# Turning blocks of the adjacency mask by DMA instead of on TensorE, with the mask applied in two VectorE operations

## The chip, the cores and the metric

The kernel runs on one core of a Trainium2 chip. The metric is the device time of one execution in microseconds. TensorE (PE) multiplies matrices and turns tiles; VectorE (DVE), ScalarE (ACT) and GpSimd (POOL) work elementwise; SyncE (SP) has no arithmetic and issues DMAs. Each engine runs its own list of instructions in order; semaphores tie the lists together.

## The reference, cut to what matters

Sixteen graphs of 1024 nodes with 128 features each go through two layers. The first is a gated graph network of four steps: messages by the adjacency matrix, then a GRU cell on every node, and a normalised residual. The second is a GraphSAGE network of three layers on a *thinned* adjacency matrix, and another normalised residual. The thinning is sequential by rows:

```python
def step(carry, n):
    row = jnp.take(carry, n, axis=0)
    num = jnp.sum(row); sf = jnp.where(num > 10, (num + 1) // 2, 1)
    rank = jnp.cumsum(row)
    rm = row & (rank % sf == 0)        # nothing is removed where num <= 1
    carry = carry.at[n].set(row & ~rm)
    carry = carry.at[:, n].set(carry[:, n] & ~rm)   # the same entries of column n
    return (carry, None)
```

What row n removes at column m is also removed at row m, column n. So row m needs, before its own entries are ranked, everything that earlier rows removed in column m.

## The kernel before, in words

The first stage, some 1290 us of the 2233, does two things side by side. `Gated` runs the gated network in two streams of graphs (a stream per parity) and its layers call a function `aside` at fixed places; each call lets `FixPoint.steps` go on to its next `yield`. So the order in which the two jobs' instructions stand on each engine is written out by hand: nothing moves when a duration changes. The rest of the time is the three GraphSAGE layers (`Sage`), which read the thinned adjacency.

`FixPoint` thins four graphs at a time (G = 4). A *round* i is one block of 128 rows, k = 0 to 7, of these four graphs; 32 rounds make the stage, and two layers of `Gated` pass in each. For a round, GpSimd has loaded the four row blocks as `f_a` (128 x 1024, bf16). Then:

- `turn` (L719) brings what older row blocks removed in these columns. For older blocks 0 to k-2 that comes back from HBM: `read_back` (L708) has read the 128x128 blocks into `f_rt` one round earlier, on SP's queue, and TensorE turns each of them (L726) into `f_tr`, which is in PSUM. Block k-1 was made in this round and is still in SBUF as `f_nr` (`fresh`), and is turned in the same way. All k blocks of a graph go to the same columns of `f_tr`, graph after graph.
- `keep` (L728) multiplies `f_a` by the sign of the turned blocks, in one VectorE `scalar_tensor_tensor` (L731) over k x 128 columns with one input in PSUM.
- `count` (L734) is a running sum along the row (L739), then parameters, three guesses of what is removed within the diagonal block (L893, L900, L908), and in the next round the final `f_nr` of all 1024 columns (L870, L872), stored to `e_nr` in HBM (L873).

The four calls of `turn` and `keep` in a round stand at fixed steps; the four `read_back` for the next round are called between those for graphs 2 and 3. Buffers: `f_rt` has 4 (pool `f_rts`), `f_tr` is one PSUM tile of one bank whose last 128 columns also hold small numbers.

Beside this, TensorE runs `Gated`'s message matmuls (L1096, on `h_a`, the adjacency that GpSimd's queue loads) and gate matmuls (L1108), and turns h (L1041); VectorE combines gates (L1121, L1123, L1136) and checks a loaded block `h_test` (L998, L1992); GpSimd multiplies gates (L1131, L1135, L1137) and issues the loads of `f_a` (L687).

Of the kernel before, what the change touches and what calls it, by code (L numbers as in the profile page):

```python
# [9 lines left out]
BF = mybir.dt.bfloat16  # L10
# [5 lines left out]
ALU = mybir.AluOpType  # L16
# [5 lines left out]
P = 128  # L22
# [3 lines left out]
NB = N // P  # L26
# [29 lines left out]
class Dilate:  # L56
# [152 lines left out]
    def steps(self):  # L209

        for b in range(B):
            self.load(0, b)
            yield 3.0
        for k in range(NB):
            self.start_chain(k)
            for t in range(P):
                self.chain_step(k, t)
                yield 1.9
            self.end_chain(k)
            x = {}  # L220
            for i in range(B + 3):
                if i < B:
                    x[i] = self.rank(k, i)
                if 1 <= i <= B:
                    self.remove(k, i - 1, x.pop(i - 1))
                if i >= 3 and k + 1 < NB:
                    self.load(k + 1, i - 3)
                yield 5.0
# [402 lines left out]
class FixPoint:  # L631
# [76 lines left out]
    def read_back(self, i, g):  # L708

        if i >= len(self.todo) or self.todo[i][0] < 2:  # L710
            return
        k, b0 = self.todo[i]
        k1 = k - 1
        rt = self.rts.tile([P, NB - 2, P], BF, name="f_rt")
        self.nc.sync.dma_start(rt[:, :k1, :], self.not_r[b0 + g, :k1 * P, k * P:k * P + P]
                               .rearrange("(j p) n -> p j n", p=P))
        self.left[i, g] = rt

    def turn(self, i, g):  # L719

        k = self.todo[i][0]
        if k:
            rt = self.left.pop((i, g), None)
            for j in range(k):
                src = rt[:, j, :] if j < k - 1 else self.fresh[g][:, k * P:k * P + P]
                self.nc.tensor.transpose(self.tr[:, j, :], src, self.cst["ident_b"])  # L726

    def keep(self, i, a):  # L728
        k = self.todo[i][0]
        if k:  # L730
            self.nc.vector.scalar_tensor_tensor(a[:, :k * P], self.tr[:, :k, :].rearrange("p k n -> p (k n)"),  # L731
                                                0.0, a[:, :k * P], op0=ALU.is_ge, op1=ALU.mult)

    def count(self, i, g, a, rank, other):  # L734
        nc = self.nc
# [6 lines left out]
    def steps(self):  # L742

        nc, G = self.nc, self.G
        for c in range(G):
            self.load(c)
        old = None
        for i, (k, b0) in enumerate(self.todo):
            diag = slice(k * P, k * P + P)

            yield
            if old:
                old.settle()
                old.wide_u(0)
            yield
            if old:
                old.wide_u(1)
                old.rows(0)
            yield
            if old:  # L760
                old.wide_u(2)
                old.rows(1)
            yield
            if old:
                old.rows(2)
                old.wide_u(3)
                old.rows(3)
            a = [self.loaded.pop((i, g)) for g in range(G)]
            pt = self.ps.tile([P, G, P], F32, name="f_pd")
            turned = pt.rearrange("p g n -> p (g n)").bitcast(BF)[:, :G * P].rearrange("p (g n) -> p g n", g=G)  # L770
            for g in range(G):
                nc.tensor.transpose(turned[:, g, :], a[g][:, diag], self.cst["ident_b"])
            yield
            if old:
                old.last_u()

            both = self.small.tile([P, G, P], BF, name="f_both")
            for g in range(G):
                nc.vector.tensor_mul(both[:, g, :], a[g][:, diag], turned[:, g, :])
            nc.gpsimd.affine_select(both, both, pattern=[[0, G], [1, P]], compare_op=ALU.is_gt, fill=0.0,  # L780
                                    base=0, channel_multiplier=-1)
            self.turn(i, 0)
            yield
            rank = self.two.tile([P, G, N], F16, name="f_rank")
            self.keep(i, a[0])
            self.count(i, 0, a[0], rank, pt)
            yield
            yield
            self.turn(i, 1)
            self.keep(i, a[1])  # L790
            yield
            self.count(i, 1, a[1], rank, pt)
            if i == 0:

                for c in range(G, self.LOTS):
                    self.load(c)
            yield
            yield
            yield
            self.turn(i, 2)  # L800
            self.keep(i, a[2])
            self.count(i, 2, a[2], rank, pt)
            yield
            for g in range(G):
                self.read_back(i + 1, g)
            yield
            self.turn(i, 3)
            self.keep(i, a[3])
            self.count(i, 3, a[3], rank, pt)

            num = self.sm[:, 0, 0, :]
            nc.vector.tensor_scalar(num, rank[:, :, N - 1], 1.0, None, op0=ALU.mult)
            q = self.params(num, 0)
            u = self.diag_u(rank[:, :, diag], q)
            if old:
                old.check()
                for g in range(G):
                    self.load(G * (i - 1) + g + self.LOTS)
            yield
            x = self.removed(u, q, both)  # L820
            yield
            yield
            pd, num = self.less(x, rank, 1)
            rd = self.small.tile([P, G, P], F16, name="f_rd")
            q = self.params(num, 1, lambda: nc.vector.tensor_sub(rd, rank[:, :, diag], pd))
            u = self.diag_u(rd, q)
            yield
            x = self.removed(u, q, both)
            yield
            old = self.Block(self, i, a, rank, both, x)  # L830
            yield
        yield
        old.settle()
        for n in range(4):
            old.wide_u(n)
            if n < 3:
                yield
            old.rows(n)
        yield
        old.last_u()  # L840
        yield
        old.check()
# [81 lines left out]
class Gated:  # L924
# [215 lines left out]
    def run(self, steps):  # L1140

        streams = [self.stream(s) for s in range(2)]
        first, second = streams
        first.load_x(first.b)
        self.load_weights()
        next(steps)
        for j in range(NB):
            first.load_adj(first.b, j)
        first.begin_rows(first.b)
        self.prepare()  # L1150
        second.load_x(second.b)
        for j in range(NB):
            second.load_adj(second.b, j)

        first.begin(0)
        for n in range(9):
            next(steps)
        for b0 in range(0, B, 2):
            for l in range(L0):
                for s in range(2):  # L1160
                    st, ot = streams[s], streams[1 - s]
                    self.layer(st, l, self.beside(st, ot, l, s, b0, steps))
        last = streams[1]
        for f in range(2):
            last.finish(f)
        for _ in steps:
            pass
# [910 lines left out]
```

## Time and profile before

| | |
|---|---|
| Median of 3 runs | 2233.61 us (2232.93 to 2242.04) |
| The profiled execution, its own time | 2232.83 us |
| Its span, first to last instruction | 2230.8 us |
| TensorE busy | 2129.7 us (95%) |
| VectorE busy | 1926.9 us (86%) |
| ScalarE busy | 1327.2 us (59%) |
| GpSimd busy | 1082.6 us (49%) |
| L726 on TensorE, `f_rt` and `f_nr` | 336 and 112 instructions |
| L731 on VectorE | 112 instructions, 265 to 1083 ns |
| L715 on SP's queue | 96 DMAs, 32 to 192 KB |

Lines of the profile name an engine, a kernel line, an operation and what it writes and reads (`out<-in`, with partitions x elements and type). A number in brackets is the idle time of the engine just before, and the arrow what ended it. A busy TensorE is not TensorE at its peak, as the ends of matmuls are modelled; the distance of starts is the surer measure.

### The profile page before, as it was taken

To read this page: it belongs to the slowest core of one execution; us is meant where nothing else is said; L and a number is where in the kernel's file an instruction comes from. 1 tells how busy PE (TensorE), PEld (TensorE's weight loads), DVE (VectorE), ACT (ScalarE), POOL (GpSimd) and SP (SyncE) were. 2 spreads that over 40 slices of the span, in tenths; PEclk is the share of its full clock that TensorE was granted. 3 is DMA by queue.
4 is the path that set the end of the run, shared out by engine and by line. 5 is a ranking of instruction groups with operands and counts; after the bars stand their busy time and mean duration, and the time that the engine had idled before them with its cause. 6 is when DMAs were issued, how large, how long until landed. Compare 5 with 4: busy or idle time off the path is not lost. (4 is left out here: it accounts for less than half of the span.)

```text
span 2230.8 us, 33341 instructions
## 1 busy us (share of the span) xinstructions
PE 2129.7 (95%) x10665; PEld 1456.6 (65%) x10665; DVE 1926.9 (86%) x4338; ACT 1327.2 (59%) x3238; POOL 1082.6 (49%) x1092
## 2 busy tenths in 40 slices
PE   6999999999999999999999979999999899998987
PEld 4566655666656666555665557777777678887865
DVE  4999999999998999999999978888888766666877
ACT  3657557565565656556566465666666455556756
POOL 4347437356355364364463346777777344551002
PEclk9999999999999999999999989999999999999989
DMA  8247347347356265364383259888888577765404
GB/s 251 71 103 240 80 114 229 71 120 214 86 156 177 73 200 138 90 201 118 73 264 85 64 184 329 305 305 297 305 301 304 169 259 260 257 221 174 152 29 144
DMA packets 214396, 402.46 MB, mean 180 GB/s; under 512 B 59586, under 2 KB 80740, under 8 KB 214212
## 3 DMA queue, kind: packets, MB, share of 16 engines
q1 hardware_dynamic: 168388, 280.68, 37.3%
q0 software_dynamic: 41472, 117.46, 19.3%
q10 hardware_dynamic: 4352, 2.11, 0.4%
q8 instruction: 86, 1.41, 0.3%
q14 instruction: 98, 0.80, 0.1%
HBM read 324.49 MB, written 109.25 MB: 194 GB/s over the span
## 5 line engine op out<-in xcount | busy, mean ns | idle before, releaser
L1108 PE MATMUL h_g<-h_h,h_wh 128*128 128x512 f32 x768 | 399.2, 601 | 3.1 <-DVE h_r L1121 3.1
L1108 PE MATMUL h_g<-h_ms,h_wi 128*128 128x512 f32 x768 | 392.1, 592 | 0.0
L739 DVE TENSOR_TENSOR_SCAN f_rank<-f_a,f_first,f_pd 128x1024 f16<-128x1024 bf16 x128 | 299.2, 2343 | 3.3
L1137 POOL TENSOR_TENSOR h_h<-h_zh,h_r 128x512 f32<-128x512 f32 x126 | 205.3, 1629 | 195.2 <-DVE h_r L1136 172.2
L1096 PE MATMUL h_g<-h_a,h_hi 128*128 128x512 f32 x1024 | 282.8, 417 | 2.2 <-DMA h_a<-in_adj_dram 2.0
L1108 PEld LDWEIGHTS h_g<-h_ms,h_wi 128*128 128x128 f32 x768 | 145.6, 190 | 183.9 <-issue 166.8
L1096 PE MATMUL h_g<-h_a,h_lo 128*128 128x512 f32 x1024 | 264.1, 395 | 0.0
L1513 POOL CAST p_b<-p_at 128x512 uint8<-128x512 f32 x256 | 219.4, 879 | 84.2 <-DVE p_at L1505 59.8
L1096 PEld LDWEIGHTS h_g<-h_a,h_hi 128*128 128x128 f32 x1024 | 188.4, 188 | 63.8 <-issue 20.1
L1096 PEld LDWEIGHTS h_g<-h_a,h_lo 128*128 128x128 f32 x1024 | 190.0, 188 | 39.4
L1406 ACT ACTIVATE s_junk<-s_o 128x128 bf16<-128x128 f32 x384 | 114.0, 298 | 170.7 <-DVE s_o L1399 170.7
L1131 POOL TENSOR_TENSOR h_zh<-h_z,h_h 128x512 f32<-128x512 f32 x63 | 80.1, 1271 | 275.5 <-ACT h_z L1127 275.5
L1108 PEld LDWEIGHTS h_g<-h_h,h_wh 128*128 128x128 f32 x768 | 129.2, 190 | 85.9 <-issue 65.5
L1099 ACT COPY h_ms<-h_g 128x512 f32<-128x512 f32 x128 | 73.8, 577 | 183.3 <-PE h_g L1096 139.3
L1124 ACT ACTIVATE h_r<-h_r,h_bi 128x512 f32<-128x512 f32 x128 | 92.3, 721 | 131.2 <-DVE h_r L1123 131.1
L916 ACT ACTIVATE f_u<-f_rank,f_q 128x128 f16<-128x128 f16 (+7 forms) x128 | 110.6, 867 | 74.9 <-DVE f_rank L856 74.9
L1992 DVE SCALAR_TENSOR_TENSOR p_junk<-p_a 128x1024 bf16<-128x1024 f32 x96 | 125.7, 1309 | 0.0
L893 ACT ACTIVATE f_pd<-f_rank,f_q 128x128 f32<-128x128 f16 x128 | 59.1, 461 | 109.8 <-DVE f_q L701 106.6
L1781 PE MATMUL q_ob<-s_wxp,q_xt 128*128 128x256 f32 x512 | 123.4, 385 | 0.3
L1505 DVE SCALAR_TENSOR_TENSOR p_at<-p_nr,p_u 128x128 fp32r<-128x128 bf16 (+1 forms) x192 | 102.5, 543 | 20.5 <-ACT p_at L1497 15.0
L1492 PE MATMUL p_u<-ident_b,p_nr 128*128 128x128 bf16 x1024 | 97.2, 224 | 7.2 <-DVE p_at L1505 5.0
L1423 POOL TENSOR_TENSOR q_rl<-s_r,q_rh 128x512 fp32r<-128x512 f32 x32 | 41.1, 1285 | 128.0 <-ACT q_rh L1422 105.5
(260 smaller groups left out, 4946.3 us busy)
## 6 DMA issues: line engine op xcount, KB each, us to landing
h_a<-in_adj_dram POOLq DMA_DIRECT2D x128, 512.0 KB, 9.5
p_a<-in_adj_dram SPq DMA_DIRECT2D x96, 512.0 KB
f_a<-in_adj_dram POOLq DMA_DIRECT2D x128, 256.0 KB, 6.6
e_nr<-f_nr SPq DMA_DIRECT2D x128, 256.0 KB
p_nr<-e_nr SPq DMA_DIRECT2D x32, 1024.0 KB
h_test<-in_adj_dram SPq DMA_DIRECT2D x32, 512.0 KB
s_at<-p_b SPq DMA_DIRECT2D x32, 512.0 KB
s_ag<-s_ag SPq DMA_DIRECT2D x64, 256.0 KB
```

The source lines that it names most:

```text
L739: nc.vector.tensor_tensor_scan(out, a, other[:, 0, 0:1].to_broadcast([P, N]), start, op0=ALU.add, op1=ALU.bypass)
L916: nc.scalar.activation(u[:, :n1], rank[:, g, :n1], AF.Abs, bias=q[:, 1, g:g + 1], scale=q[:, 0, g:g + 1])
L1096: nc.tensor.matmul(pm[f], part[:, j, :], st.adj[j][:, half[f]], start=(j == 0 and n == 0), stop=(j == NB - 1 and n == 1))
L1108: nc.tensor.matmul(pg, lhs, rhs, start=(i == 0), stop=(i == len(mm) - 1))
L1124: nc.scalar.activation(r, r, AF.Tanh, bias=bias(self.bi, 2))
L1137: aid.tensor_tensor(h, zh, r, ALU.subtract)
L1406: self.nc.scalar.activation(junk, o[:, i, :], AF.Square, accum_out=ss[:, i:i + 1])
L1492: nc.tensor.matmul(pu[:, i * P:(i + 1) * P], v[:, 4 * f + i, j * P:(j + 1) * P], self.cst["ident_b"], start=True, stop=True)
L1505: self.nc.vector.scalar_tensor_tensor(g["at"][:, j, c0:c0 + low], v[:, j, c0:c0 + low], 0.0, pu[:, :low], op0=ALU.is_lt, op1=ALU.is_lt)
L1513: self.nc.gpsimd.tensor_copy(g["b", f][:, j, :], g["at"][:, j, f * HF:(f + 1) * HF].bitcast(F32))
L1781: nc.tensor.matmul(pb[:, i], g["xt"][:, f, blk], self.wxp, start=(i % 2 == 0), stop=False)
L1992: nc.vector.scalar_tensor_tensor(junk, a, 0.0, a, op0=ALU.is_gt, op1=ALU.not_equal, accum_out=bad[:, c:c + 1])
```

## The change

The older blocks are turned on their way from HBM: `read_back` issues one transposing DMA per graph from SP, which writes the k-1 blocks to `f_rt` already turned. TensorE turns only block k-1, into a slot of `f_tr` of its own per graph. `keep` applies the mask in two operations: columns of blocks 0 to k-2 with `f_rt` in SBUF as the second input, columns of block k-1 with `f_tr` in PSUM. Rounds with k = 0 and 1 have no older blocks. In the changed file the kernel's lines from here on stand one lower.

```diff
         k1 = k - 1
-        rt = self.rts.tile([P, NB - 2, P], BF, name="f_rt")
-        self.nc.sync.dma_start(rt[:, :k1, :], self.not_r[b0 + g, :k1 * P, k * P:k * P + P]
-                               .rearrange("(j p) n -> p j n", p=P))
+        rt = self.rts.tile([P, (NB - 2) * P], BF, name="f_rt")
+        self.nc.sync.dma_start(rt[:, :k1 * P], self.not_r[b0 + g, :k1 * P, k * P:k * P + P], transpose=True)
         self.left[i, g] = rt

     def turn(self, i, g):

         k = self.todo[i][0]
         if k:
-            rt = self.left.pop((i, g), None)
-            for j in range(k):
-                src = rt[:, j, :] if j < k - 1 else self.fresh[g][:, k * P:k * P + P]
-                self.nc.tensor.transpose(self.tr[:, j, :], src, self.cst["ident_b"])
-
-    def keep(self, i, a):
-        k = self.todo[i][0]
+            self.nc.tensor.transpose(self.tr[:, g, :], self.fresh[g][:, k * P:k * P + P], self.cst["ident_b"])
+
+    def keep(self, i, g, a):
+        k, stt = self.todo[i][0], self.nc.vector.scalar_tensor_tensor
         if k:
-            self.nc.vector.scalar_tensor_tensor(a[:, :k * P], self.tr[:, :k, :].rearrange("p k n -> p (k n)"),
-                                                0.0, a[:, :k * P], op0=ALU.is_ge, op1=ALU.mult)
+            last = slice((k - 1) * P, k * P)
+            if k > 1:
+                rt = self.left.pop((i, g))
+                stt(a[:, :(k - 1) * P], rt[:, :(k - 1) * P], 0.0, a[:, :(k - 1) * P], op0=ALU.is_ge, op1=ALU.mult)
+            stt(a[:, last], self.tr[:, g, :], 0.0, a[:, last], op0=ALU.is_ge, op1=ALU.mult)
...
-            self.keep(i, a[0])
+            self.keep(i, 0, a[0])
```

The other three calls of `keep` change in the same way.

More of the change, by code (lines that the diff above doesn't have):

```diff
@@ L789, in steps @@
             self.turn(i, 1)
-            self.keep(i, a[1])
+            self.keep(i, 1, a[1])
             yield
@@ L800, in steps @@
             self.turn(i, 2)
-            self.keep(i, a[2])
+            self.keep(i, 2, a[2])
             self.count(i, 2, a[2], rank, pt)
@@ L807, in steps @@
             self.turn(i, 3)
-            self.keep(i, a[3])
+            self.keep(i, 3, a[3])
             self.count(i, 3, a[3], rank, pt)
```

## The prediction

> **What bounds the kernel now.** I read the page's 40 slices first: TensorE is busy 90% or more in every slice of the first 1290 us (the stage that the change touches), but VectorE stands at 9 there too. A busy share can't separate two engines that are both full, so I cut one group of four graphs into its eight rounds (k = 0 to 7). Each window starts where the round's L772 transposes start on TensorE.
>
> ```profile
> 655.20:696.00 40.80, 40.16 (x157) 24.47 (x156) 36.33 (x70) 27.45 (x58) 34.09 (x38) 1.00 0.84 271
> 696.00:734.40 38.40, 38.40 (x146) 23.13 (x146) 36.42 (x78) 22.85 (x42) 14.79 (x14) 1.00 0.30 72
> 734.40:773.00 38.60, 38.60 (x150) 23.33 (x150) 36.45 (x78) 22.39 (x41) 14.29 (x14) 1.00 0.30 76
> 773.00:811.80 38.80, 38.80 (x154) 23.54 (x154) 36.99 (x78) 22.29 (x41) 16.42 (x18) 1.00 0.47 132
> 811.80:852.70 40.90, 40.90 (x173) 25.17 (x172) 37.39 (x74) 28.08 (x61) 33.48 (x38) 1.00 0.89 283
> 852.70:892.40 39.70, 39.48 (x161) 24.01 (x160) 38.37 (x78) 22.62 (x42) 14.72 (x14) 1.00 0.34 83
> 892.40:932.40 40.00, 39.73 (x166) 24.25 (x166) 38.63 (x78) 22.39 (x41) 14.47 (x14) 1.00 0.35 86
> 932.40:972.90 40.50, 40.19 (x170) 24.39 (x170) 39.20 (x76) 22.36 (x40) 16.54 (x18) 1.00 0.40 117
> ```
>
> Columns: window, its length, then busy us of TensorE, its weight loads, VectorE, ScalarE, GpSimd, clock, DMA share, GB/s. To see: at k = 1, 2, 3 the length is TensorE's busy time. By the L772 starts (696.01, 734.38, 772.97, 811.79) these rounds take 38.37, 38.59 and 38.82 us, so one more row block costs 0.22 to 0.23. In k = 5, 6, 7 (39.69, 39.97, 40.49) the length is above TensorE's line (38.37 + 0.23 each would give 39.29, 39.52, 39.75), TensorE idles 0.2 to 0.3 us, and VectorE idles only 1.33, 1.37 and 1.30 us, which is the sum of small gaps between some 78 instructions. There VectorE sets the length. So the stage has two owners: TensorE to k = 4, VectorE from k = 5.
>
> What a transpose really costs is the distance of starts, in the TensorE timeline of round 6, not its 220 ns:
>
> ```profile
> 902.51 0.44 PE L726 MATMUL f_tr<-ident_b,f_rt 128*128 128x128 bf16 x5
> 902.79 0.22 PE L726 MATMUL f_tr<-ident_b,f_nr 128*128 128x128 bf16 x1
> 902.85 0.65 PE L1108 MATMUL h_g<-h_h,h_wh 128*128 128x512 f32 x1
> ```
>
> Six take 902.85 - 902.51 = 0.34 us: 57 ns each, and 4 x 57 = 0.23 us per row block, the step found above.
>
> The mask on VectorE, from the groups by shape:
>
> ```profile
> L731 DVE SCALAR_TENSOR_TENSOR f_a<-f_tr,f_a 128x768 bf16<-128x768 bf16 x16 | 15.1, 941 | 0.0
> L731 DVE SCALAR_TENSOR_TENSOR f_a<-f_tr,f_a 128x128 bf16<-128x128 bf16 x16 | 4.5, 280 | 1.4 <-PE f_tr L726 1.2
> L886 DVE SCALAR_TENSOR_TENSOR f_junk<-f_x 128x512 f16<-128x512 bf16 x31 | 21.5, 692 | 1.1
> ```
>
> (941 - 280) / 640 = 1.03 ns an element, plus 0.147 us fixed. L886 is the same operation with both inputs in SBUF: 692 ns for 512, against 680 for L731 at 512 from PSUM. Neither the place nor the 16-bit type makes it cheaper.
>
> A second cost, of place. L1992 is one instruction in two stages, from the answer for its tile and line; below it the third mask of round 6 and GpSimd beside it:
>
> ```profile
> L1992 DVE SCALAR_TENSOR_TENSOR p_junk<-p_a x96: 1204/1214/1831, 1334.0 to 1775.3; 128x1024 bf16<-128x1024 f32 x96
> L1992 DVE SCALAR_TENSOR_TENSOR h_junk<-h_test x32: 1626/1644/2171, 58.1 to 1290.3; 128x1024 bf16<-128x1024 f32 x32
> 908.85 1.29 POOL L1135 TENSOR_TENSOR h_zh<-h_z,h_h 128x512 f32<-128x512 f32 x1
> 909.92 0.93 DVE L731 SCALAR_TENSOR_TENSOR f_a<-f_tr,f_a 128x768 bf16<-128x768 bf16 x1
> 910.23 1.29 POOL L1137 TENSOR_TENSOR h_h<-h_zh,h_r 128x512 f32<-128x512 f32 x1
> ```
>
> In the first stage the least L1992 takes 1626 ns instead of 1204: it starts 0.4 us before a GpSimd L1135 ends, each time. The mask at 909.92 has one input in PSUM and pays nothing beside the same L1135.
>
> Last, SP's queue in round 6:
>
> ```profile
> 894.22 3.94 SPq L873 DMA_DIRECT2D e_nr<-f_nr  x4
> 898.28 14.96 SPq L715 DMA_DIRECT2D f_rt<-e_nr  x4
> 913.28 0.54 SPq L998 DMA_DIRECT2D h_test<-in_adj_dram  x1
> ```
>
> The reads for round 7 go out one by one as their buffers come free and are used 39 us later; h_test is behind them on the queue.
>
> **What the Trainium skill says.** "SBUF — State Buffer", Who interferes with whom: a VectorE instruction with two SBUF inputs and a GpSimd instruction that reads SBUF exclude each other for the whole instruction; with one SBUF input there is no contention. The trace agrees (1626 against 1204). "Vector Engine (DVE) Microarchitecture Reference", Performance modes, lists copy, cast, tensor_scalar and tensor_tensor for the packed modes and not scalar_tensor_tensor; L886 at 692 ns agrees. "DMA: Bandwidth & Descriptors", Queues, rings and completion order: each DMA engine takes a queue's descriptors in ring order; no row here shows it by itself. Prices of a DMA transpose: 1309 ns for 128x128 bf16 ("VectorE: DVE Perf Modes", The three transpose paths) and 261 GB/s (the DMA page, Latency and other measured facts). This trace has no DMA transpose.
>
> **The change part by part**, per round k >= 2, four graphs each.
>
> *TensorE* loses 4 x (k - 1) transposes: 0.23, 0.46, 0.69, 0.92, 1.15, 1.38 us for k = 2 to 7. Over the stage 336 x 57 ns = 19.2 us, which is a gain only where TensorE sets the length.
>
> *VectorE* gets a second operation per mask. Elements stay; the fixed part comes once more, 0.147 us, less the overlap of two independent operations: two L1136 of 0.684 us take 1.28, so 0.083. Four times 0.064 = 0.26 us. The first of the two has both inputs in SBUF: the third graph's mask always meets L1135 (909.92 against 908.85 + 1.29 = 910.14), wait 0.22 us. Sum 0.48 us a round. Bounds: 0.26 if the port costs nothing; 1.36 if nothing overlaps (0.59), the port costs 0.22 and one L687 issue of 0.55 us on GpSimd, which runs beside the fourth mask, shuts it out too. A gain from SBUF input is excluded by L886. I take 0.48, as each term has a row.
>
> *GpSimd's* L1137, pushed back by the third mask's 0.7 us, holds the second half of h, which TensorE turns (L1041) some 8 us later: hidden.
>
> *Waits.* The SBUF mask waits for the DMA transpose; behind it on VectorE are the scan L739 and L1121/L1123, which free the PSUM banks that TensorE's L1108 needs. SP's L715 waits for the mask instead of the transposes: 898.28 becomes about 901.3, the last about 914; behind it stand h_test and, far later, L873. TensorE's remaining transposes still wait for the mask before, as all write one bank. SP and GpSimd issue as many DMAs in the same order as before.
>
> *DMA.* A round-7 transpose moves 192 KB: 0.75 us at 261 GB/s, 7.9 us at 1309 ns per 128x128 block. Deadlines are 39 us off; four take 3 or 31 us. I take the low end as likelier, since a single small transfer's time needn't add up over blocks, and keep the high one for a rival.
>
> *Sum by round*, larger of the two engines (VectorE: busy + 1.33 + 0.48): k = 2: 38.26 against 38.37, so -0.22. k = 3: 38.80, so -0.02. k = 4: VectorE 39.20, TensorE 40.94 - 0.69, so -0.69. k = 5, 6, 7: +0.48 each, +1.44. A group +0.51 us, four groups **+2.0 us**. The profiled execution took 2232.8 (span 2230.8, 2.0 outside) and would take 2234.8; the median of the runs is 0.8 higher: **2236**.
>
> **Rivals.** *DMA transposes at 1309 ns a block.* Round 7's 24 take 31.4 us from 901.3, to 932.7; h_test behind them, 512 KB at the page's 180 GB/s, lands at 935.6, and VectorE's L1992 wants it at about 930.1 (37.7 us after the round's start, as in round 5). 5.5 us late, 22 in all: 2258. Where DMA is 0.89 busy (k = 4) another 21 us of transposes could hold up the h_a loads, up to 16 us a group: 2323. I put it at 2265. It decides from 1.08 us a block ((930.1 - 2.9 - 901.3) / 24). For it: the price; against it: the 261 GB/s. *The port costs its upper bound,* 1.36 us a round: +0.56, +0.85, -0.69 and three times +1.36 are 4.8 a group, 19 in all: 2253. *TensorE's saving arrives whole:* 2214, the other side. It needs VectorE to have slack in k = 5 to 7, and 1.3 us spread over gaps speaks against it.
>
> **How the numbers follow.** The balance as summed 0.45 (own range 2228 to 2244), slow transposes 0.33, costly port 0.14, whole saving 0.08. A measurement of this kernel tells about 0.5%, 11 us. Faster is the last case: 0.07. Same is the first and crumbs of others: 0.47. Slower is the two between: 0.46. The range 2226 to 2300 leaves out some 0.05 below and 0.13 above, where transposes hold up h_a.
>
> **What would show it.** Right: rounds 1 to 4 shorter by 0, 0.2, 0 and 0.7 us, rounds 5 to 7 longer by 0.5; the SBUF mask at 810 ns for 640 elements except in the third graph, 0.2 more; no VectorE idle ahead of it. Wrong: VectorE idle before the SBUF mask or L1992 released by a DMA, TensorE idle before L1096 released by h_a, SBUF masks far above 1.03 ns an element, or rounds 5 to 7 that shorten.

## The result and the profile after

The changed kernel takes 2246.06 us (median of 20 runs, 2239.56 to 2254.27), against 2235.40 us (2232.93 to 2242.04, 20 runs) for the kernel before on the same chips. The ratio is 1.0047, with a 95% interval of 1.0037 to 1.0057: slower by 10.7 us. The forecast was 2236. The runs of the changed kernel also spread over 14.7 us, those of the kernel before over 9.1. The profiled execution is one at the slow end: 2254.27 us, span 2252.5.

The windows by round, first of the same group of four graphs as before (k = 1 to 7), then the fourth round (k = 4) of the first group. Columns as before: window, length, then busy us of TensorE, its weight loads, VectorE, ScalarE and GpSimd, clock, DMA share, GB/s.

```profile
708.21:746.57 38.36, 38.36 (x145) 23.09 (x145) 35.53 (x78) 22.11 (x42) 13.93 (x14) 1.00 0.29 72
746.57:784.93 38.36, 38.36 (x145) 23.09 (x145) 36.81 (x82) 22.51 (x41) 14.40 (x14) 1.00 0.31 76
784.93:823.76 38.83, 38.58 (x146) 23.13 (x145) 37.39 (x82) 22.46 (x41) 16.62 (x18) 1.00 0.48 132
823.76:865.61 41.85, 40.45 (x162) 24.43 (x161) 37.52 (x76) 27.57 (x60) 33.93 (x38) 1.00 0.97 277
865.61:906.37 40.76, 39.10 (x146) 22.96 (x145) 39.20 (x84) 23.12 (x42) 15.55 (x14) 1.00 0.37 81
906.37:946.83 40.46, 38.82 (x146) 23.00 (x145) 39.09 (x82) 22.48 (x41) 14.99 (x14) 1.00 0.38 85
946.83:987.70 40.87, 38.88 (x146) 23.10 (x145) 39.58 (x80) 22.37 (x40) 17.13 (x18) 1.00 0.40 116
...
175.92:222.50 46.58, 41.89 (x161) 25.16 (x161) 43.53 (x78) 28.64 (x61) 34.62 (x38) 0.96 0.80 248
```

Three things are to be seen. k = 2 lost its 0.23 us. In k = 5 to 7 TensorE now idles 1.6 to 2.0 us of each round, where it idled 0.2 to 0.3, and VectorE's idle time is still 1.3 to 1.6: VectorE sets those rounds, and they grew; only the rounds 5 behind the two longest rounds 4 did not (39.68 and 39.67 us, against 39.69 to 39.71 before). And round 4, forecast to shrink by 0.69 us, did so nowhere: it took 40.93 to 41.85 us in two groups (before: 40.72 to 41.14) and 46.23 and 46.58 in the other two.

The first stage, from the first to the last start of a round, went from 1218.35 us to 1234.62 between the two profiled executions. What follows that stage took 978.6 and 985.0 us there; over all the profiles of this study it lies between 978.6 and 985.9, in kernels as fast as before too (984.1 in one of them), so single profiles are compared by the stage below, and times by medians of runs.

**The stall in round 4.** DVE and POOL timelines of the first group, then TensorE's:

```profile
182.74 0.69 DVE L1122 TENSOR_TENSOR h_r<-h_g,h_r 128x512 f32<-128x512 f32 x1
183.35 6.98 DVE L730 SCALAR_TENSOR_TENSOR f_a<-f_rt,f_a 128x384 bf16<-128x384 bf16 x1
190.25 0.28 DVE L731 SCALAR_TENSOR_TENSOR f_a<-f_tr,f_a 128x128 bf16<-128x128 bf16 x1
...
183.15 0.66 POOL L779 TENSOR_SCALAR_AFFINE_SELECT f_both<-f_both 128x512 bf16<-128x512 bf16 x1
183.76 1.28 POOL L1073 TENSOR_TENSOR h_x<-h_x,h_w 128x512 f32<-128x512 f32 x1
184.99 2.48 POOL L1060 TENSOR_TENSOR h_lo<-h_x,h_hi 128x512 fp32r<-128x512 f32 x2
187.44 1.25 POOL L1130 TENSOR_TENSOR h_zh<-h_z,h_h 128x512 f32<-128x512 f32 x1
188.66 1.25 POOL L1073 TENSOR_TENSOR h_x<-h_x,h_w 128x512 f32<-128x512 f32 x1
190.21 0.60 POOL L1075 DMA_DIRECT2D e_sum<-h_x  x1 [0.30 <-POOL h_x L1073]
...
190.59 0.25 PE L722 MATMUL f_tr<-ident_b,f_nr 128*128 128x128 bf16 x1 [4.69 <-DVE f_a L731]
190.64 2.01 PE L1107 MATMUL h_g<-h_h,h_wh 128*128 128x512 f32 x2
```

The first graph's SBUF mask (L730, both inputs in SBUF) takes 6.98 us instead of 0.55; this is called a stall below. GpSimd meanwhile runs a select (L779) and then, back to back, five products of two SBUF tensors, until 188.66 + 1.25 = 189.91; the mask ends 0.4 us after that. TensorE's second turn waits for the PSUM mask behind it, and TensorE idles for 4.69 us. In the next 3.4 us it has half its clock:

```profile
190.60:194.00 3.40, 3.40 (x5) 1.38 (x5) 3.26 (x3) 0.00 (x0) 0.21 (x1) 0.51 1.13 420
```

The second group has the same (mask 6.70 us, TensorE idle 4.34). In the third and fourth the first mask took 0.55 us.

**The waits that grew.** From the chain of waits (engine, line, what it waited for: us in all, times, longest):

```profile
PE h_g L1040 <- ACT h_r L1117: 14.7, 12, 1.7
PE f_tr L722 <- DVE f_a L731: 9.0, 2, 4.7
...
PE h_g L1095 <- DMA h_a<-in_adj_dram: 4.4, 6, 1.4
```

The first is new and is TensorE waiting in rounds 5 to 7 for VectorE's late gates, by way of ScalarE. The second is the two stalls. The third was smaller in the kernel before:

```profile
PE h_g L1096 <- DMA h_a<-in_adj_dram: 2.0, 4, 0.8
```

No row has VectorE waiting for a DMA ahead of L730 or L1991: the transposes are always in time.

**The masks by shape**, from the groups of VectorE (count, busy us, mean ns, idle before):

```profile
L731 DVE SCALAR_TENSOR_TENSOR f_a<-f_tr,f_a 128x128 bf16<-128x128 bf16 x112 | 31.5, 281 | 3.5 <-PE f_tr L722 3.4
L730 DVE SCALAR_TENSOR_TENSOR f_a<-f_rt,f_a 128x384 bf16<-128x384 bf16 x16 | 23.1, 1443 | 0.0
L730 DVE SCALAR_TENSOR_TENSOR f_a<-f_rt,f_a 128x768 bf16<-128x768 bf16 x16 | 15.5, 969 | 0.0
L730 DVE SCALAR_TENSOR_TENSOR f_a<-f_rt,f_a 128x640 bf16<-128x640 bf16 x16 | 13.4, 835 | 0.0
```

640 columns take 835 ns on the mean of four graphs (810 forecast, and 0.2 more in the third graph, which is 0.05 on the mean). 384 columns stand out. The third graph's mask in round 6 and the GpSimd product beside it:

```profile
924.13 0.91 DVE L730 SCALAR_TENSOR_TENSOR f_a<-f_rt,f_a 128x640 bf16<-128x640 bf16 x1
...
923.06 1.29 POOL L1134 TENSOR_TENSOR h_zh<-h_z,h_h 128x512 f32<-128x512 f32 x1
```

It arrives 0.22 us before L1134 ends, as forecast, and takes 0.91 us where the masks of the other three graphs take 0.80 to 0.82: the wait is seen as 0.1 us. The turns on TensorE and the check L1991:

```profile
916.18 0.22 PE L722 MATMUL f_tr<-ident_b,f_nr 128*128 128x128 bf16 x1
916.24 1.08 PE L1107 MATMUL h_g<-h_h,h_wh 128*128 128x512 f32 x2
...
L1991 DVE SCALAR_TENSOR_TENSOR p_junk<-p_a x96: 1204/1212/1853, 1349.4 to 1792.9; 128x1024 bf16<-128x1024 f32 x96
L1991 DVE SCALAR_TENSOR_TENSOR h_junk<-h_test x32: 1631/1644/2177, 57.2 to 1306.0; 128x1024 bf16<-128x1024 f32 x32
```

One turn is left, 0.06 us by starts. L1991 is what it was. SP's queue in round 6, then the DMAs of L715 by themselves (minimum, median, maximum ns on SP):

```profile
915.23 14.37 SPq L715 DMA_TRANSPOSE f_rt<-e_nr  x4
929.65 0.62 SPq L997 DMA_DIRECT2D h_test<-in_adj_dram  x1
...
L715 SPq DMA_TRANSPOSE f_rt<-e_nr x96: 1104/1138/1971, 65.9 to 1249.1; - x96
```

The four reads go out from 8.86 us after the round's start (before: 5.86), as forecast, and h_test behind them 23.3 us after it (20.9 before). Each issue costs SP 1138 ns instead of 370; SP has the time.

### The profile page after: what moved, and what is told of

Read it like the earlier page. It is cut to its first block, busy times and chain, and to the rows that moved or that the text cites. A ratio compares the mean times of both kernels' runs of the same rounds, so it can differ in the third digit from the quotient of the medians.

```text
span 2252.5 us, 32765 instructions
## 1 busy us (share of the span) xinstructions
PE 2122.0 (94%) x10329; PEld 1440.0 (64%) x10329; DVE 1947.5 (86%) x4434; ACT 1327.8 (59%) x3238; POOL 1092.3 (48%) x1092
## 5 line engine op out<-in xcount | busy, mean ns | idle before, releaser
L1136 POOL TENSOR_TENSOR h_h<-h_zh,h_r 128x512 f32<-128x512 f32 x126 | 212.7, 1688 | 208.7 <-DVE h_r L1135 196.2
L1095 PE MATMUL h_g<-h_a,h_hi 128*128 128x512 f32 x1024 | 282.5, 417 | 4.4 <-DMA h_a<-in_adj_dram 4.4
L1095 PE MATMUL h_g<-h_a,h_lo 128*128 128x512 f32 x1024 | 263.9, 395 | 0.0
L1095 PEld LDWEIGHTS h_g<-h_a,h_hi 128*128 128x128 f32 x1024 | 188.6, 189 | 65.4 <-issue 22.0
L1095 PEld LDWEIGHTS h_g<-h_a,h_lo 128*128 128x128 f32 x1024 | 189.9, 188 | 39.5
L1991 DVE SCALAR_TENSOR_TENSOR p_junk<-p_a 128x1024 bf16<-128x1024 f32 x96 | 125.7, 1309 | 0.0
L1040 PEld LDWEIGHTS h_g<-ident,h_h 128*128 128x128 f32 x512 | 60.3, 141 | 75.1 <-issue 68.3
```

The lines of the kernel that those rows point to most:

```text
L1095: nc.tensor.matmul(pm[f], part[:, j, :], st.adj[j][:, half[f]], start=(j == 0 and n == 0), stop=(j == NB - 1 and n == 1))
L1136: aid.tensor_tensor(h, zh, r, ALU.subtract)
L1991: nc.vector.scalar_tensor_tensor(junk, a, 0.0, a, op0=ALU.is_gt, op1=ALU.not_equal, accum_out=bad[:, c:c + 1])
```

## The experiments

Versions of the kernel are compared with the kernel before by runs on the same chip. "Stage" is again the time from the first to the last start of a round in the one profiled execution, 1218.35 us in the kernel before.

**The change again.** The same kernel, for a second profile.

> The changed kernel again, beside the others. Theory (port): the time is that of the balance, some 5 us over before, plus 5 to 6 us for every round 4 in which the SBUF mask L730 is shut out for about 6.5 us by GpSimd's run of L1073, L1060, L1060, L1130, L1073. So 2241 + 5.5 times the number of L730 over 5 us; with one such on average 2246. Each one also shows TensorE idle of more than 4 us before L722, released by L731. Rival (DMA): the excess doesn't follow the number of long L730.

2244.83 us (2241.07 to 2251.51, 7 runs) against 2236.66; ratio 1.0045 (1.0027 to 1.0062). The profile has one stall, in the third group, for which the expectation gives 2246.5 us; this execution took 2244.83. The stage is 1230.33 us. The mask and GpSimd's first two instructions beside it, then TensorE in the first group's round 7, and a window behind that wait (columns as above):

```profile
823.29 6.78 DVE L730 SCALAR_TENSOR_TENSOR f_a<-f_rt,f_a 128x384 bf16<-128x384 bf16 x1
...
822.89 0.65 POOL L779 TENSOR_SCALAR_AFFINE_SELECT f_both<-f_both 128x512 bf16<-128x512 bf16 x1
823.50 1.28 POOL L1073 TENSOR_TENSOR h_x<-h_x,h_w 128x512 f32<-128x512 f32 x1
...
325.66 0.63 PE L1040 MATMUL h_g<-ident,h_h 128*128 128x128 f32 x4 [1.71 <-ACT h_r L1117]
...
327.50:330.90 3.40, 3.40 (x6) 1.40 (x5) 2.92 (x12) 3.20 (x7) 1.27 (x1) 0.52 0.58 212
```

The stall comes and goes with the execution: 3 of the 8 fourth rounds of two profiles have it. A pattern holds in all 8: the three stalled masks start 0.17 to 0.46 us before the end of the select L779, the other five start at most 0.09 us before that end, or after it. The last two lines are a second effect: in two of the three seventh rounds inside this stage, TensorE's clock fell by half after the 1.71 us wait for h_r, and these rounds took 42.60 and 42.71 us instead of 40.9. The three seventh rounds of the first profile have the same wait and kept their clock, so the wait alone does not decide it; what does is not shown.

**The port by itself.** A kernel in which VectorE does one mask of 128x384 while GpSimd multiplies.

> A small program that computes nothing of the reference: it times one VectorE instruction of 128x384 bf16 beside runs of GpSimd products of 128x512 f32, three times over. Cases in order: no run; 3, 6 and 12 independent products; a chain of 6, each reading the one before; then beside 6 independent ones: the mask with one input in PSUM, a tensor_tensor with both in SBUF, a tensor_scalar from SBUF. Theory (starved at the port): the SBUF mask waits for the end of the whole independent run, some 0.55 us alone and then about 2.5, 6 and 13 us; in the chain, whose members leave gaps, it slips in at the next gap, 1 to 2 us; from PSUM 0.55 us. Rival (turns are taken): it waits for one GpSimd product at most in every case, 0.55 to 1.9 us.

Beside 3, 6 and 12 products back to back (each of one tensor with itself, 1.04 us) the mask took 1.36 us, whatever the number (once 0.72); from PSUM 0.55. The theory fell here: VectorE waited for one product and no more; in the chain, whose products leave gaps, it took 0.55 us. But these products read one tensor twice, and the kernel's read two.

```profile
19.62 1.36 DVE L105 SCALAR_TENSOR_TENSOR w_a<-w_r,w_a 128x384 bf16<-128x384 bf16 x1
...
18.53 6.34 POOL L98 TENSOR_TENSOR w_o<-w_src 128x512 f32<-128x512 f32 x6 [1.47 <-DVE w_src L88]
```

**Two inputs.** The same with products of two tensors, with and without a select ahead.

> A kernel that computes nothing of the reference: it measures one VectorE mask of 128x384 bf16 beside GpSimd's work, eight cases, three times each. Cases in order: 5 GpSimd products of two different SBUF tensors behind an affine_select, mask arriving 0.3 us or 0.7 us after GpSimd starts; the same without the select; 10 products without the select; 5 products of one tensor with itself, without and with the select; the first case with the mask's other input in PSUM. Theory (back-to-back GpSimd products of two tensors keep VectorE out until their run ends): 5 to 6.5 us for the mask in the cases with 5 products of two tensors, over 10 us with 10, about 1.4 us with products of one tensor, 0.55 us from PSUM. Second form of it (only a mask that is already waiting through a select is passed over): 5 to 6.5 us in the first case alone. Rival (they take turns): 1.3 to 2 us in every case from SBUF, and then the 7 us of the fourth round have another cause.

1.31 us in the cases in which the mask met a product, with 5 products and with 10 (1.08 with one tensor); 1.66 us at most. So the first form of the theory fell: a run of products of two tensors doesn't keep the mask out. The second form was not tested, because the select waited for nothing and was over before the mask came. A third kernel put the mask into the select:

> A kernel that computes nothing of the reference: again one VectorE mask of 128x384 bf16 beside GpSimd's work, now arriving while GpSimd is in an instruction with one input. Nine cases, three times each: a select and 5 products of two tensors, mask 0.2 us before the select's end; the same with 10 products; with 5 products of one tensor with itself; with the mask's other input in PSUM; mask arriving after the select's end, in the first product; mask arriving 0.3 us before the select's end; a tensor_scalar in place of the select; a product in its place; and a select with one product only. Theory (a mask that arrives while GpSimd is in an instruction with one input, which doesn't shut it out, is passed over by every product that follows back to back): over 6 us in the first and sixth case, over 12 us with 10 products, 0.55 us from PSUM, 1.0 to 1.6 us in the fifth and eighth, some 2 us in the last, and over 6 us behind the tensor_scalar too, if it is the one input that counts and not the select. Rival (turns are taken, however it arrives): 0.5 to 2 us in all nine.

```profile
26.08 0.64 POOL L102 TENSOR_SCALAR_AFFINE_SELECT w_both<-w_both 128x512 bf16<-128x512 bf16 x1 [1.93 <-DVE w_both L92]
26.25 0.87 DVE L115 SCALAR_TENSOR_TENSOR w_a<-w_r,w_a 128x384 bf16<-128x384 bf16 x1
26.68 12.54 POOL L112 TENSOR_TENSOR w_o<-w_src,w_t 128x512 f32<-128x512 f32 x10
```

0.87 us, though 10 products follow; 0.67 to 1.00 in the other selects, 1.41 at most anywhere, 0.55 from PSUM. The theory fell again, and the rival held in all nine cases: by itself, VectorE's mask waits for no more than the one instruction that it meets. The arrival in a select that goes with every stall of the kernel is not enough to make one.

**The first mask of round 4 turned by TensorE.** The variants below share one edit of the changed kernel, and differ in the condition:

```diff
+        if self.by_pe(k, g):
+            self.nc.sync.dma_start(rt[:, :k1 * P].rearrange("p (j n) -> p j n", n=P), src.rearrange("(j p) n -> p j n", p=P))
+        else:
+            self.nc.sync.dma_start(rt[:, :k1 * P], src, transpose=True)
...
+    def by_pe(self, k, g):
+        return (k, g) == (4, 0)
```

Where it holds, TensorE turns all blocks, and `keep` is one operation from PSUM, as before.

> The changed kernel, but for one mask of each group: graph 0 of round 4 is read plainly, turned on TensorE and masked in one operation from PSUM, as before. Four masks of 96. Theory (port): it takes away the mask that meets GpSimd's run, so the stalls of 5 us go: no L730 over 2.5 us, 2240 to 2242, and less scatter than the changed kernel. Rival (the second operation, or DMA): nothing much changes, 2245 to 2247.

2243.71 us (2238.59 to 2245.03, 7 runs), ratio 1.0036 (1.0023 to 1.0048); stage 1222.35. No VectorE instruction of the stage takes 6 us any more, and the slowest run fell from 2251.5 to 2245.0. The median moved by 1.1 us, to 7.1 us over the kernel before, where 4 to 5 were expected.

**All of round 4 by TensorE** (`k == 4`).

> The change, but with all four masks of the fourth rounds (k = 4) turned on TensorE and applied from PSUM. Theory (the scatter of 15 us of the changed kernel is the stall of the first SBUF mask in round 4, and the rest of its loss lies in rounds 5 to 7): no VectorE instruction of 6 us, rounds 4 at 40.7 to 41.1 us, rounds 5 to 7 longer by 0 to 0.5 us each; 2 to 5 us over the kernel before, and the slowest run under 2246. Rival (the stall moves to another SBUF mask, or the clock and h_a make the loss): about 10 us over the kernel before and runs up to 2252.

2242.99 us (2236.86 to 2247.82, 15 runs) against 2235.74; ratio 1.0031 (1.0021 to 1.0041); stage 1224.19. No stall; rounds 4 at 40.78 to 41.44 us, rounds 6 and 7 at 40.35 and 40.9. So without a stall the change still costs 7 us, more than either of these two expectations had: the stall is the smaller part of the loss.

**The select behind the products.** In rounds 4 GpSimd's L779 stands behind its five products:

```diff
-            nc.gpsimd.affine_select(both, both, ...)
+            if k != 4:
+                select()
...
             yield
             yield
+            if k == 4:
+                select()
             self.turn(i, 1)
```

> The change, but in the fourth rounds (k = 4) GpSimd's affine_select stands behind its five products (two L1073, two L1060, one L1130) instead of ahead of them; nothing else is moved. Theory (the 7 us come from the mask's arriving during the select): no VectorE instruction of 6 us; the first SBUF mask of round 4 meets a product and takes 0.55 to 1.9 us; rounds 4 at 40.7 to 42 us; 5 to 9 us over the kernel before, as with that mask turned on TensorE, and the slowest run under 2249. Rival (any arrival ahead of the five products is passed over): the mask now arrives in the run every time, so it takes 5 us or more in most of the four groups, and the kernel takes 2252 to 2265.

The third group's mask and products (L1077 and L1064 are L1073 and L1060 four lines on):

```profile
823.73 0.55 DVE L730 SCALAR_TENSOR_TENSOR f_a<-f_rt,f_a 128x384 bf16<-128x384 bf16 x1
...
823.74 1.67 POOL L1077 TENSOR_TENSOR h_x<-h_x,h_w 128x512 f32<-128x512 f32 x1 [0.55 <-ACT h_w L1074]
825.37 2.50 POOL L1064 TENSOR_TENSOR h_lo<-h_x,h_hi 128x512 fp32r<-128x512 f32 x2
```

No stall in any group, and five runs within 3.5 us (2245.51 to 2249.01). But the first product now waits for ScalarE and starts within 0.01 us of the mask in all four groups, so this mask never met the run of products from within. The second graph's SBUF mask of the same rounds does; the run goes on:

```profile
828.28 1.25 DVE L730 SCALAR_TENSOR_TENSOR f_a<-f_rt,f_a 128x384 bf16<-128x384 bf16 x1
...
827.83 1.29 POOL L1134 TENSOR_TENSOR h_zh<-h_z,h_h 128x512 f32<-128x512 f32 x1
829.08 1.59 POOL L1077 TENSOR_TENSOR h_x<-h_x,h_w 128x512 f32<-128x512 f32 x1
```

It arrives in the fourth product, waits for that one, and goes ahead of the fifth, which takes 1.59 us instead of 1.25. The same is seen in all 17 rounds in which an SBUF mask arrives in this fourth product: four here, five in the two profiles of the change (its rounds 4 without a stall), and eight in the versions with one mask by TensorE and with DMA in rounds 2 to 4. The masks take 0.91 to 1.26 us. So the rival falls too: it isn't any arrival ahead of a product that is passed over. The median is 2246.46, ratio 1.0054 (1.0040 to 1.0068): 10.9 us over the kernel before where 5 to 9 were expected, and slower than the round by TensorE. The later select has a price of its own: `both` is late, TensorE waits 0.8 to 1.0 us ahead of L911 in three of the four rounds 4, and these take 41.66 to 42.28 us.

**The second operation alone.** The kernel before, its mask cut in two operations, both from PSUM:

```diff
+            for lo, hi in ((0, k - 1), (k - 1, k)):
+                if lo < hi:
+                    cols = slice(lo * P, hi * P)
```

> The kernel before, with only its mask cut in two operations, both from PSUM: the second operation's fixed cost by itself, without the shared port and without DMA transposes. Theory (port): 0.26 us more in rounds 5 to 7 and nothing elsewhere, 12 x 0.26 = 3 us, so 2238 to 2239. If the second operation and not the port makes the change slow, 2244 or more.

2240.79 us (2236.61 to 2246.18, 22 runs) against 2236.66; ratio 1.0018 (1.0009 to 1.0027). Rounds 5, 6 and 7 take about 40.0, 40.3 and 40.85 us, 0.3 more each (0.26 was forecast for this part); the time is 4.1 us over the kernel before, where some 3 were expected. Over half of what the change costs without a stall is there with nothing in it but the second operation.

**Transposes that nobody reads.** The kernel before with the 96 transposing DMAs added, and then with plain reads added in their place:

```diff
+        idle = self.idle.tile([P, (NB - 2) * P], BF, name="f_idle")
+        self.nc.sync.dma_start(idle[:, :k1 * P], self.not_r[b0 + g, :k1 * P, k * P:k * P + P], transpose=True)
```

> The kernel before, with the 96 transposing DMAs added behind its own reads, into buffers that nothing reads. It has all of the change's DMA work and none of its VectorE work. Theory (port): DMA transposes are hidden, so within 3 us of before, 2235 to 2238, and no L731 over 1.1 us. Rival (DMA): they hold up h_test or the h_a loads, and the change's 10 us or more appear here, 2245 or above, with idle TensorE before L1096 released by DMA.

> The kernel before, with the 96 extra DMAs that nobody reads, as plain reads instead of transposing ones. Theory (what the idle transposes cost, 5.5 us, comes from the transposing: SP's issue of some 1.1 us instead of 0.35 us and slow writes that hold up h_a in the fourth rounds): within 1.5 us of the kernel before, TensorE's waits for h_a about 2 us in all. Rival (it is the added 10 MB of traffic where DMA is 0.89 busy): 4 to 6 us over the kernel before, waits for h_a 4 us or more.

The transposes: 2242.21 us (2238.52 to 2248.63, 17 runs) against 2236.66, ratio 1.0025 (1.0015 to 1.0034). The plain reads: 2236.87 (2232.18 to 2240.13, 14 runs) against 2235.74, ratio 1.0003 (0.9994 to 1.0012). TensorE's waits for h_a in the two, in order:

```profile
PE h_g L1099 <- DMA h_a<-in_adj_dram: 4.6, 8, 1.2
```

```profile
PE h_g L1100 <- DMA h_a<-in_adj_dram: 2.1, 5, 0.5
```

It is the transposing and not the bytes, at a price between the two expectations. In the profile with idle transposes the lengthening is all in two rounds 4, of 43.35 and 43.98 us, where h_a is late 35 to 37 us into the round. SP's slowest issues take 5.4 to 6.7 us in all four rounds 4, and the other two are no longer than before (40.95 and 40.98 us), so slow issues alone do not explain it. The changed kernel waits there for 0.1 us at most: it has transposes in place of the reads, not on top of them, so this experiment overstates its case.

**Part of the change.** DMA turns the blocks in rounds 2 to 4, without the first graph of round 4 (`(k, g) == (4, 0) or k >= 5` by TensorE); and in rounds 2 and 3 alone (`k >= 4`).

> DMA transposes only where TensorE sets the length: rounds 2, 3 and 4, without graph 0 of round 4; rounds 5 to 7 wholly as before. Theory (port, and VectorE as owner from round 5): rounds 2 to 4 gain 0.22, 0 and up to 0.5 us a group, nothing is lost: 2232 to 2236. If DMA transposes or the second operation cost where VectorE has slack, 2238 or more.

> The change in rounds 2 and 3 alone; rounds 4 to 7 by TensorE with one mask from PSUM, as before. Theory (where TensorE sets the length its saving arrives, and the waits for h_a of 1.2 and 1.8 us that rounds 4 showed with DMA in 2 to 4 come from the transposes): rounds 2 and 3 shorter by 0.22 and 0.0 to 0.4 us, rounds 4 at 40.7 to 41.1, TensorE's waits for h_a 2 us in all; 1 to 3 us under the kernel before. Rival (the transposes that round 4 itself no longer has were worth as much as they cost): equal to the version with DMA in rounds 2 to 4, or slower than it by 1 us, with the waits for h_a still there.

2233.22 us (2227.29 to 2238.00, 14 runs) against 2235.51, and 2233.63 (2230.84 to 2237.62, 13 runs) against 2235.74. Both ratios are 0.9988, with intervals of 0.9978 to 0.9997 and 0.9979 to 0.9997: the only versions that beat both kernels, by 2 us. Stages are 1217.64 and 1216.63. TensorE's waits for h_a in round 4 of the first, which sit 14.5 to 15.9 us into the round (L1115 is L1095 with the edit's lines ahead):

```profile
826.19 0.50 PE L1115 MATMUL h_g<-h_a,h_hi 128*128 128x512 f32 x1 [1.24 <-DMA h_a<-in_adj_dram]
...
1145.18 0.51 PE L1115 MATMUL h_g<-h_a,h_hi 128*128 128x512 f32 x1 [1.82 <-DMA h_a<-in_adj_dram]
```

In the second they are 0.16 to 0.57 us in three groups and none in the other. So round 4 by TensorE already has nothing to spare at this point. Neither version issues a transpose during round 4, so the two long waits of the first need another cause, and the traces show a likely one. Among the DMA queues of that last round 4, from its start to 16 us behind it, is this one (packets, MB, share of the 16 engines):

```profile
q8 instruction: 1, 0.02, 0.4%
```

The packet, of 16 KB on a queue that the profile calls "instruction", starts 13.6 us into the round, among the loads of h_a, and takes 0.93 us; the fourth block of h_a, for which TensorE waits, lands at 15.8 us. Over the eleven profiles of whole kernels such a packet comes 9 to 14 us into a round 4 seven times, and each time the fourth block is late (14.7 to 15.8 us). In 36 of the other 37 rounds 4 it has landed by 14.5 us. The exception, 15.1 us, is in the second profile of the change: there some twenty packets of the loads end together at 15.1 us, 1.9 us after SP began to issue a transpose, so that a transpose may be the cause. In the kernel before, the packet comes 21.1 to 21.6 us into all four rounds 4, too late to matter. The stage has 39 of these packets there and in the three versions that leave TensorE's instructions as they were, and 36 with the change, which takes 336 turns and their 336 weight loads from TensorE. So the change seems to shift these packets in time. All this is read from the traces; no run changes the packet alone. The medians of the two versions don't differ, so what the transposes for round 4 bring and cost can't be told apart by the times.

## Why the prediction was right, and where it was not

The number came out within the stated range, 2226 to 2300, and 10.7 us are just under the 11 us (0.5%) that the forecast took as the least difference to be told; but that is luck in good part. The balance had 2.0 us more and gave itself 2228 to 2244; the change costs 10.7 us, and 2246.06 lies above that. The range reached higher for the sake of two rivals that did not come true.

The sum by rounds, set against the profiles. In the row of k = 4 and 5, "without a stall" takes the 5 of 8 groups of the two profiles of the change that have none; the other rows take all groups, with the rounds 7 at full clock. The kernel before is the mean of its groups.

| rounds of a group | before, us | forecast | without a stall | with a stall |
|---|---|---|---|---|
| k = 1 to 3 | 115.84 | -0.24 | -0.14 | |
| k = 4 and 5 | 80.62 | -0.21 | +1.06 | +5.81 |
| k = 6 and 7 | 80.46 | +0.96 | +0.87 | |
| sum | | +0.51 | +1.79 | +6.54 |

*TensorE to k = 3: right.* k = 2 fell from 38.59 to 38.35 or 38.38 (-0.22 forecast). k = 3 scatters from 38.47 to 39.11 over the eight groups, and its mean is 38.81 against 38.82 (-0.02 forecast). The forecast had VectorE hold this round at 38.80, and two of the eight groups went below 38.5, so the agreement of the mean is partly luck.

*VectorE from k = 5: right.* The idle floor of 1.3 us stayed (1.3 to 1.6), the saved TensorE time came back as waits of TensorE, and rounds 6 and 7 grew by 0.9 together. Of the two terms of the 0.48 us, the second operation measures about 0.3 alone (0.26 forecast), the wait at the port 0.1 (0.22 forecast). The two errors nearly cancel. The second could have been read: the least L1992 starts 0.54 us before the recorded end of L1135 (not 0.4, as the prediction has it; in all 32 it is 0.54 to 1.07) and loses 0.42, so it is let in 0.12 us ahead of that recorded end, and 0.12 less than 0.22 is the 0.1 that was measured.

*Round 4: wrong.* The step that failed is "VectorE 39.20, TensorE 40.94 - 0.69, so -0.69". It let TensorE's saving arrive whole and put a wait for data at nothing. Two owners were weighed, and there is a third: the h_a blocks. In the kernel before, the fourth block lands 13.9 to 14.3 us into that round, and TensorE asks for it at 14.2. With its saved turns it asks at 13.9, and in three of the five rounds 4 without a stall it waits 0.3 to 0.5 us for a block that is on time. In the other two the block came at 15.1 and 15.2 us, and the wait was 1.3 and 1.4:

```profile
839.03 0.51 PE L1095 MATMUL h_g<-h_a,h_hi 128*128 128x512 f32 x1 [1.40 <-DMA h_a<-in_adj_dram]
```

The forecast named a late h_a only as a harm that slow transposes would do, not as a limit on the saving. The five rounds are 0.34 us longer than before on the mean, where -0.69 was forecast; 0.8 of these 1.03 us are waits for h_a, and the rest is not located. Round 5 behind them takes 39.93 to 40.76 us instead of 39.69, which is +0.72 where +0.48 was forecast. So -0.21 became +1.06 in each group, and 1.27 x 4 = 5.1 us is the larger part of the miss. The sum without a stall is 1.79 x 4 = 7.2 us against 2.0 forecast. The versions without a stall lose as much (7.1 with one mask by TensorE, 7.3 with the round by TensorE), but their profiled rounds, summed in the same way, give +1.05 and +1.27 a group, 4.2 and 5.1 us. The other 2 to 3 us of theirs are not located; one profile each, the first of them of the fastest of its runs, beside runs that spread over 6 to 11 us, can't show them.

*The port in round 4: right in place, wrong in price.* The prediction had the SBUF mask shut out for the rest of one GpSimd instruction, and saw that of the third graph alone. The first graph's mask meets L779 and five products in round 4 and is kept out of all of them in 3 cases of 8. A stall adds 5.81 - 1.06 = 4.75 us. With the 7.2 us of those two versions for the rest, 10.7 - 7.2 = 3.5 us of the result is left for stalls, which is 0.7 of a stall per run on the mean: an estimate from medians. The two profiles can't confirm it, as the price was taken from them; less 4.75 for each stall their stages are 6.8 and 7.2 us over the kernel before, and 3.5 of the second are its two rounds 7 at half clock.

What makes a stall is narrowed down, not settled. Shown: it needs the SBUF input (with the mask from PSUM no profile has one, and the slowest runs came down); in all three cases the mask arrived 0.17 to 0.46 us ahead of the select's end; a mask that arrives in a product of the same run waits for that product alone, 17 times of 17. With the select moved there was none in four rounds, which fits but is few. Not shown: why GpSimd's next five instructions went ahead of a mask that had been waiting. Three kernels made to reproduce it gave turns taken instruction by instruction. The Trainium skill, "SBUF — State Buffer", Who interferes with whom, says as much, that the one which comes second blocks until the first instruction ends; the made-up kernels and the 17 masks agree with it, the 6.98 us do not.

*The rivals.* "DMA transposes at 1309 ns a block" is out: no instruction of VectorE waited for a DMA at the mask or at L1991, and h_test went out 23.3 us into the round. In a weak form it is alive in round 4 only, where DMA is 0.8 to 0.97 busy. "The port costs its upper bound" of 1.36 us in every round is out: it is 0.1, with rare large exceptions in one round. "TensorE's saving arrives whole" is out, and its reason was the one given: VectorE has no slack from k = 5.

Of the signs that were to show it wrong, two appeared: TensorE idle ahead of the h_a matmuls, and SBUF masks far above 1.03 ns an element. They are the two places of the miss.

## What to carry to other kernels

When the engine that sets a stage gets work taken off it, look in each part of the stage for what arrives next, data included: the gain here ended at VectorE in three rounds of eight and at a load in one, and what was left was the price of a second VectorE instruction. Splitting an operation so that one half has both inputs in SBUF exposes it to GpSimd; look at what it meets at every place, not at the mean: here one place in eight rounds made the stalls. Apply such a change only where the engine that it relieves sets the length: limited to rounds 2 and 3 it gave 2 us, everywhere it cost 10.7.

## What the runs showed of the hardware that was not expected

- A VectorE mask of 0.55 us took 6.70 to 6.98 us beside a select and five products of GpSimd, in 3 executed rounds of 8, and never in the 60 SBUF masks of the three small kernels (1.66 us at most). Masks that arrived in the fourth of those products took 0.91 to 1.26 us.
- TensorE's granted clock was 0.51 for 3.4 us after it had idled 4.69 us. The Trainium skill, "TensorE: Matmul & The Clock Gate", Part 1, has half the clock after an idle window of about 3.4 us, which agrees. It was 0.52 for 3.4 us also after a wait of only 1.71 us, shorter than that window, in two of the 15 rounds 7 with this wait in the stages of five profiles, and that made them 1.7 us longer.
- A DMA transpose took SP 1138 ns to issue (a plain read of the same blocks 370), and up to 6.7 us in the rounds 4 of the kernel with idle transposes (DMA share 0.96 to 1.07 there).
- 96 transposes that nobody reads cost 5.5 us; 96 plain reads of the same bytes cost 1.1, within the noise.
- A block of h_a that TensorE was next to ask for (the fourth) landed 0.6 to 1.7 us later than in the kernel before (14.1 us on the mean) in each of the seven rounds 4 in which a 16 KB packet of queue q8 fell among its loads.
